# Order of the stores of weight sums in SP's queue, and a PSUM bank for each of the last two token tiles, in a float32 cross-attention block

## The chip, the cores and the metric

The kernel runs on one core of one Trainium2 chip. The metric is the device time of one execution in microseconds, as the median of several executions. A core has five engines with a queue each: TensorE (PE in the profile), VectorE (DVE, `V` in the code), ScalarE (ACT), GpSimd (POOL, `GP` in the code) and SyncE (SP), which here issues the DMAs. Within a queue instructions go in order, and between queues they wait for semaphores. Matrix products land in PSUM[...]; everything else is in SBUF.

## The reference

A transformer block on 8 sequences of 256 tokens with 512 channels: a layer norm, cross-attention with 16 heads of 32 channels on 256 encoder tokens, and a two-layer perceptron with 2048 hidden channels, all in float32. The mask is all true. The change lies in the perceptron:

```python
hidden = out + residual
residual = hidden
y = layer_norm(hidden, ln2_w, ln2_b)
y = jax.nn.gelu(y @ fc_w + fc_b, approximate=True)
y = y @ proj_w + proj_b
return residual + y
```

## The kernel before

The 2048 tokens are cut into four groups of 512 (`g` = 0 to 3). First come attention stages for all groups, with the projections of the next group laid between. Then the perceptron runs group by group (the loop at L1027). Every large product is done by a Strassen scheme with seven products of half-sized blocks in place of eight. Operands carry sums and differences of their four quarters, `11`, `12`, `21`, `22`: for weights these are `s3`, `s2`, the new `21`, and `s4` (`A_SUMS`, L155), and for tokens `t1`, `t2`, the new `12`, and `t4` (`B_SUMS`, L161). In the trace the tiles `fcw` of the first weights are called `w` or `fcw`, and all elementwise sums have the line of the helper `add`, L929; matmuls have that of `mm`, L926.

Group 0 differs from the others. Its first layer (hidden sums `pf`) runs in four quarters `q` = 0 to 3 of the hidden channels with one Strassen level (L1131 to L1200). In each quarter TensorE does the products in the order `11`, `s2`, `s3`, `21`, `12`, `22`, `s4`. They go into the PSUM banks 1, 6, 7, 5, and the last three accumulate again in banks 1, 7 and 5. VectorE and ScalarE take partial results out: `u1` is a copy on ScalarE, `u2` = bank 6 + `u1`, `u3` = bank 7 + `u2`. So product `22`, which accumulates in bank 7, has to wait until `u3` has been read out of that bank, and product `s4` until the sum `x["22"]` = bank 5 + `u3` is done. The sums `x["12"]` and `x["21"]` follow, and Gelu runs on ScalarE.

Groups 1 to 3 use a second Strassen level on the first-layer weights. The extra weight sums are made once, in group 0, beside its products, and are kept in DRAM (`w2_dram`): that is `split_sums` (L965). For a weight quarter or sum `n` and a half `r` of the columns it makes four sums `s1` to `s4` from `fcw[r]` and `fcw[r + 2]`, on VectorE or GpSimd as its first argument says. They go into one of three staging slots (`stage`, `w_stage` in the trace), used in turn, and then two DMAs on SP take them to DRAM (L979 for `s1`, L980 for the other three). A slot may be written again when the DMAs that read it have landed. With `half` 0 only the first two sums are made; with `half` 1 the other two, and then the DMAs are issued. The order is written by hand: the table `SPLITS` (L1116) says which calls come at which point `(q, at)`, and the function `splits` goes through it. A call puts its sums into its engine's queue and its two DMAs into SP's queue at that point, so SP's order is the order of the calls. Point 0 comes after `u2`, point 1 after `u3`, point 2 after `x["22"]`, and point 3 after `x["12"]`. GpSimd makes, beside its share of these sums, the sums `h` for the projection (`sum_h`) at the end of each quarter, and the roots for the next group's layer norm. The slots of `11`, `12`, `s2`, `s3`, `21`, `s4`, `22` for r = 0 are 0, 1, 2, 0, 1, 2, 0; for r = 1, `11`, `12`, `s2` take 1, 2, 0.

After the four quarters comes the projection (`py`) with seven products of 32 recorded matmuls each, from L1316: `11` into bank 1, `s3` into bank 7, then turns of the next group's tokens, then `12`, `21`, `12` with `22`, `11` with `t1`, and `22` with `t4`, which accumulates in bank 7. A bank holds two token tiles, `bank[:, 0, :]` and `bank[:, 1, :]`. In the last group the product into bank 7 at the very end is done tile by tile, so that the store of the first tile can leave before the second is done:

```python
for i in range(2):
    proj(bank[7], "22", "t4", False, True, (i,))
    o = ht[:, 2 + i, :HD2]
    add(V, o, bank[7][:, i, :], o)
    store(1, slice(HD2), (i,))
```

Of the kernel before, what the change touches and what calls it, by code (L numbers as in the profile page):

```python
# [10 lines left out]
F32 = mybir.dt.float32  # L11
# [5 lines left out]
P = 128  # L17
# [5 lines left out]
def tile_xattn_block(  # L23
# [52 lines left out]
    NG = B // GB  # L76
    G = GB * S
# [8 lines left out]
    HI, HC, HF, HD2 = INNER // 2, NC // 2, NF // 2, D // 2  # L86
# [165 lines left out]
    with ExitStack() as att:  # L252
# [5 lines left out]
        ps_m = att.enter_context(tc.tile_pool(name="ps_m", bufs=1, space=PSUM))  # L258
# [169 lines left out]
        def project_qk(g, tag):  # L428
            w, base = ("k", c_kb) if tag == "kT" else ("q", c_qb)

            def made(n, bank, u):
                o, k = int(n[0]) - 1, int(n[1]) - 1

                direct = g == 0 and o == 0
                st = None if direct else staged(g, tag, n)
                for i in range(2):
                    b = col(base, 2 * o + i)
                    to = qk[g, i, tag][:, ts(k, S)] if direct else st[:, i, :]
                    if u is None:
                        nc.scalar.activation(to, bank[:, i, :], AF.Identity, bias=b, scale=1.0)  # L440
                    else:
                        nc.vector.scalar_tensor_tensor(
                            to, bank[:, i, :], b, u[:, i, :], ALU.add, ALU.add
                        )
                if not direct:
                    store_quarter(g, tag, o, k, st)

            def src():
                return (ctxT if tag == "kT" else xnT)[g]

            if g == 0:
                for i in range(2):
                    qk[g, i, tag] = work.tile([P, G], F32, tag=tag, name=f"{tag}_{g}_{i}")
            if g == 0 and tag == "kT":
                return [lambda n=n: eight(f"p{tag}_{g}", n, ws[w], src, made, FIRST_KEYS.get(n, {})) for n in QUARTERS]
            return strassen(f"p{tag}_{g}", lambda: ws[w], src, False, made)
# [255 lines left out]
        V, GP = nc.vector, nc.gpsimd  # L712
# [53 lines left out]
        g = 1  # L766
        begin(g, 0, 3, load_res, 0, *QUARTERS)
        begin(g, 2, 2, bias_res, 0)
        g = 2
# [6 lines left out]
        g = NG - 1  # L776
# [55 lines left out]
        k, q, v, tx = project_qk(0, "kT"), project_qk(0, "qT"), project_v(0), turn_x(0)  # L832
# [63 lines left out]
        o = project_out(3)  # L896
# [11 lines left out]
    with ExitStack() as mlp:  # L908
# [5 lines left out]
        ps_m = mlp.enter_context(  # L914
            tc.tile_pool(name="ps_mm", bufs=2, space=PSUM, reuse_waits="tile")
        )
        NQF = HF // 2
        V, GP = nc.vector, nc.gpsimd
# [9 lines left out]
        def add(eng, to, a, b, op=ALU.add):  # L928
            eng.tensor_tensor(to, a, b, op)  # L929
# [97 lines left out]
        for g in range(NG):  # L1027
# [13 lines left out]
            def bank_of(n, name):  # L1041
                return ps_f.tile(
                    [P, 2, S], F32, tag=f"f{n}", bufs=2 if n in (1, 5) else 1, name=f"{name}_{g}"
                )
# [57 lines left out]
            if g == 0:  # L1102
                y = ys[g]

                def fc(bank, w, b, q, first, last):
# [9 lines left out]

                SPLITS = {  # L1116
                    (2, 0): ((GP, "11", 0), (V, "12", 0, 0)),
                    (2, 1): ((GP, "s2", 0), (V, "12", 0, 1)),
                    (2, 2): ((V, "s3", 0, 0), (GP, "21", 0)),
                    (2, 3): ((V, "s3", 0, 1),),  # L1120
                    (3, 0): ((GP, "s4", 0), (V, "22", 0, 0)),
                    (3, 1): ((GP, "11", 1), (V, "22", 0, 1)),
                    (3, 2): ((V, "12", 1, 0), (GP, "s2", 1)),
                    (3, 3): ((V, "12", 1, 1),),
                }

                def splits(q, at):
                    for args in SPLITS.get((q, at), ()):
                        split_sums(*args)

                for q in range(NQF):  # L1131
                    bank = {n: bank_of(n, f"pf{n}_{q}") for n in (1, 6, 7, 5)}
                    u1, u2, u3 = (us(n, f"u{n}_{q}") for n in (1, 2, 3))
                    x = {n: h[n][:, :, 2 * q : 2 * q + 2, :] for n in h}

                    def by_h(t):
                        return t.rearrange("p i (d s) -> p d i s", d=2)

                    def gelu(n, half, src):
                        for i in range(2):  # L1140
                            nc.scalar.activation(
                                x[n][:, :, i, :],
                                src[:, :, i, :],
                                AF.Gelu_apprx_tanh,
                                bias=col(c_fcb, half * HF + 2 * q + i),
                                scale=1.0,
                            )

                    def some_pw(n):
                        for _ in range((0, n, n // 2, n // 2)[q]):  # L1150
                            next(pw_sums)

                    fc_sums = [(1, 0), (1, 1), (1, 2), (1, 3)] if q == 0 else []
                    fc_sums += [(q + 2, i) for i in range(4)] if q + 2 < NQF else []

                    def some_fc_sums(n):
                        for at, i in fc_sums[:n]:
                            sum_up(GP, fcw[at], A_SUMS, i)
                        del fc_sums[:n]

                    fc(bank[1], "11", "11", q, True, False)
                    nc.scalar.copy(u1, bank[1])
                    fc(bank[6], "s2", "t2", q, True, True)
                    add(V, u2, bank[6], u1)
                    splits(q, 0)
                    fc(bank[7], "s3", "12", q, True, False)
                    add(V, u3, bank[7], u2)
                    splits(q, 1)
                    fc(bank[5], "21", "t1", q, True, False)
                    add(V, x["22"], by_h(bank[5]), by_h(u3))  # L1170
                    some_fc_sums(4)
                    some_pw(2)
                    splits(q, 2)
                    fc(bank[1], "12", "21", q, False, True)

                    gelu("11", 0, by_h(bank[1]))
                    gelu("22", 1, x["22"])
                    fc(bank[7], "22", "t4", q, False, True)
                    add(V, x["12"], by_h(bank[7]), by_h(u2))
                    splits(q, 3)  # L1180
                    some_norm(q, 0, 1, 1, 0)
                    some_fc_sums(4)
                    some_pw(2)
                    gelu("12", 1, x["12"])
                    fc(bank[5], "s4", "22", q, False, True)
                    add(V, x["21"], by_h(bank[5]), by_h(u2))
                    some_norm(q, 0, 1, 2, 1)
                    gelu("21", 0, x["21"])
                    sum_h("s3", q)
                    sum_h("s2", q)  # L1190
                    if q == 0:
                        ht = residual(work, hid_dram[g], "resm", f"resm_{g}")
                        load_next()
                    if q >= 1:
                        keep_quarters(q)
                    if q == 1:
                        keep_quarters(0)
                    if q == 3:
                        bias_ht()
                        normalise_next()  # L1200
# [114 lines left out]

            bank = {n: bank_of(n, f"py{n}") for n in (1, 7, 6, 5)}  # L1316

            def proj(bank, a, w, first, last, tiles=(0, 1)):
                for i in tiles:
                    for p in range(HF):  # L1320
                        mm(
                            bank[:, i, :],
                            h[a][:, i, p, :],
                            pw[w][:, p, :],
                            first and i == 0 and p == 0,
                            last and p == HF - 1,
                        )

# [14 lines left out]
            u1, u2, u3 = (us(n, f"v{n}") for n in (1, 2, 3))  # L1343
# [28 lines left out]
                    next(pw_sums)  # L1372
            proj(bank[6], "21", "t2", True, True)
            add(V, u2, bank[6], u1)
            add(V, u3, bank[7], u2)
            for b, k, u in ((0, 1, u2), (1, 1, u3), (1, 0, u2)):
                o_add(GP, b, k, u)
            if g == 0:
# [13 lines left out]
            if g + 1 < NG:  # L1392
                split_y(g + 1)
                proj(bank[7], "22", "t4", False, True)
                o_add(V, 1, 0, bank[7])
                store(1)
            else:

                store(1, slice(HD2, D))
                for i in range(2):  # L1400
                    proj(bank[7], "22", "t4", False, True, (i,))
                    o = ht[:, 2 + i, :HD2]
                    add(V, o, bank[7][:, i, :], o)
                    store(1, slice(HD2), (i,))


# [39 lines left out]
```

## Time and profile before

| what | us |
|---|---|
| median of 3 runs | 741.91 (741.21 to 742.51) |
| the profiled execution, its own time | 741.43 |
| its span in the profile | 739.7 |
| stage: group 0, first layer (`pf`) | 346.4 to 405.2 |
| stage: group 0, projection (`py`) | 405.2 to 455.3 |
| stage: groups 1 to 3 | 455.3 to 736.2 |

The span is the time that the hardware profiler shows; the execution's own time has 1.7 us more around it. Times in profile lines count from the start of the span. A timeline line has the start, the length, the engine, the line of the kernel, the operation, what it writes and reads, and in brackets how long the engine was idle before it and what ended that. "SPq" is the issue of a DMA on SP's queue. In the trace a float32 matmul of the code is two records, so a product of four matmuls is "x8".

### The profile page before, as it was taken

The page shows a single profiled execution, that of the slowest core. Times are in us where ns is not written, and L with a number is a line of the kernel's source. Part 1 is how long each engine was busy: PE and PEld are TensorE (multiplying, and loading weights), DVE is VectorE, ACT ScalarE, POOL GpSimd, SP SyncE. Part 2 cuts the span into 40 slices and gives each one's busy share as a digit, 9 for nine tenths or more (in the row PEclk, how much of TensorE's full clock was granted, in tenths as well). Part 3 has the DMA queues.
Part 4 walks back from the last instruction along what each step waited for, and adds up shares of the span by engine and source line. Part 5 has one row for each costly group of instructions (what it writes and reads, how often), then busy time and mean ns, then how long its engine had stood idle before and what let it go on. Part 6 is the DMA issues. An engine that isn't in the chain of part 4 may idle for free.

```text
span 739.7 us, 13634 instructions
## 1 busy us (share of the span) xinstructions
PE 725.8 (98%) x4941; PEld 627.5 (85%) x4941; DVE 407.2 (55%) x1055; ACT 312.4 (42%) x888; POOL 478.8 (65%) x441
## 2 busy tenths in 40 slices
PE   8999999999999999999996999999999999999997
PEld 7888788888778777778885889998899988999886
DVE  4676756666456567856466295681156811566111
ACT  2277788766676787850322200226002160031500
POOL 3857779677554479996847970489504896048960
PEclk9999999999999999999998999999999999999999
DMA  9714522642234268434965791992019930172001
GB/s 299 246 58 141 160 92 97 199 150 73 86 107 156 85 201 263 154 105 128 339 231 177 253 358 58 370 338 104 1 58 336 346 129 1 58 272 84 1 1 57
DMA packets 79714, 117.82 MB, mean 159 GB/s; under 512 B 6644, under 2 KB 58400, under 8 KB 77984
## 3 DMA queue, kind: packets, MB, share of 16 engines
q1 hardware_dynamic: 79392, 116.94, 46.1%
q8 instruction: 39, 0.64, 0.4%
q14 instruction: 27, 0.22, 0.1%
q0 software_dynamic: 256, 0.02, 0.0%
HBM read 85.48 MB, written 31.46 MB: 158 GB/s over the span
## 4 chain that ended last, share of the span: by engine, by line
PE 92%; DMA 3%; SPq 1%; POOL 1%; DVE 1%; issue 0%; ACT 0%; DVEq 0%; POOLq 0%
PE py L926 26%; PE pf L926 19%; PE ppt L628 8%; PE pv L370 7%; PE po L370 7%; PE pqT L370 7%; PE pkT L370 5%; PE s L575 5%; PE av L644 4%; PE pkT L467 2%; DMA hm<-hid_dram 1%; DMA w_dram<-w_stage 1%; PE pyt L217 1%; PE pxt L217 1%; POOL w_stage L929 1%; SPq L935 1%
## 5 line engine op out<-in xcount | busy, mean ns | idle before, releaser
L617 POOL TENSOR_TENSOR pr<-pr,rsum 128x512 f32<-128x512 f32 x128 | 130.2, 1051 | 68.7 <-DVE rsum L615 39.9
L929 POOL TENSOR_TENSOR h<-h,hs 128x512 f32<-128x512 f32 x79 | 98.8, 1273 | 105.0 <-DVE hs L929 104.4
L603 ACT ACTIVATE pr<-pr,nmax 128x256 f32<-128x256 f32 x256 | 127.8, 502 | 37.4 <-DVE nmax L593 37.1
L926 PEld LDWEIGHTS pf<-y,w 128*128 128x128 f32 x1176 | 131.8, 192 | 0.2
L926 PE MATMUL pf<-y,w 128*128 128x128 f32 x1176 | 131.8, 275 | 0.0
L593 DVE CUSTOM_DVE_ANT_0 pr<-s,mb 128x256 f32<-128x256 f32 x256 | 93.5, 413 | 39.7 <-PE s L575 29.9
L926 PE MATMUL py<-pw_t,h 128*128 128x256 f32 x384 | 84.5, 379 | 0.6 <-DVE resm L929 0.6
L926 PE MATMUL py<-pw,h 128*128 128x256 f32 x384 | 84.9, 379 | 0.0
L926 PEld LDWEIGHTS py<-pw_t,h 128*128 128x128 f32 x384 | 72.6, 190 | 10.7 <-DVE resm L929 1.0
L926 PEld LDWEIGHTS py<-pw,h 128*128 128x128 f32 x384 | 72.5, 190 | 9.6
L1267 ACT COPY u<-pf 128x512 f32<-128x512 f32 x21 | 12.3, 585 | 161.1 <-PE pf L926 161.1
L628 PEld LDWEIGHTS ppt<-ident,pr 128*128 128x128 f32 x512 | 57.5, 141 | 14.6 <-issue 9.3
L628 PE MATMUL ppt<-ident,pr 128*128 128x128 f32 x512 | 68.5, 276 | 0.2
L929 DVE TENSOR_TENSOR resm<-py,resm 128x512 f32<-128x512 f32 (+1 forms) x21 | 13.6, 663 | 85.5 <-PE py L926 85.5
L926 PE MATMUL pf<-y,fcw 128*128 128x256 f32 x224 | 52.0, 393 | 7.0 <-DVE u L929 6.6
L926 PEld LDWEIGHTS pf<-y,fcw 128*128 128x128 f32 x224 | 43.8, 197 | 15.1 <-DVE u L929 7.4
L633 ACT COPY pt<-ppt 128x512 f32<-128x512 f32 x96 | 51.8, 573 | 7.1 <-PE ppt L628 7.1
L370 PE MATMUL pv<-vw,ctxT 128*128 128x256 f32 x224 | 52.4, 380 | 0.0
L929 DVE TENSOR_TENSOR u<-pf,u 128x512 f32<-128x512 f32 x50 | 34.5, 690 | 30.9 <-PE pf L926 26.6
L370 PE MATMUL pqT<-xnT,qw 128*128 128x256 f32 x224 | 51.0, 379 | 0.0
L603 ACT ACTIVATION_READ_ACCUMULATOR pr<-pr,nmax 128x1 f32 x256 | 48.8, 191 | 0.0
L370 PEld LDWEIGHTS pqT<-xnT,qw 128*128 128x128 f32 x224 | 41.4, 190 | 5.0
(142 smaller groups left out, 1134.8 us busy)
## 6 DMA issues: line engine op xcount, KB each, us to landing
w<-w_dram SPq DMA_DIRECT2D x12, 1792.0 KB, 7.6
w<-in_L_xattn_fc_w_dram SPq DMA_DIRECT2D x27, 256.0 KB, 5.1
w<-w_dram SPq DMA_DIRECT2D x9, 768.0 KB, 7.1
w_dram<-w_stage SPq DMA_DIRECT2D x14, 384.0 KB, 3.1
ctx<-in_ctx_dram SPq DMA_DIRECT2D x16, 256.0 KB, 4.0
x<-in_x_dram SPq DMA_DIRECT2D x16, 256.0 KB, 4.9
v_dram<-st_v SPq DMA_DIRECT2D x16, 256.0 KB, 2.2
v<-v_dram SPq DMA_DIRECT2D x16, 256.0 KB, 3.6
```

What stands on the lines that cost most here:

```text
L217: nc.tensor.transpose(ps[:, ts(t, P)], xt[:, ts(c, P)], ident)
L370: nc.tensor.matmul(bank[n][:, i, :], l[:, c, ts(i, P)], r[:, c, :], start=first and i == 0 and c == 0, stop=last and c == HC - 1, skip_gro ...
L467: nc.tensor.matmul(bank[:, i, :], w[f"{n[0]}{j + 1}"][:, c, ts(i, P)], x()[f"{j + 1}{n[1]}"][:, c, :], start=at == 0, stop=j == 1 and c == ...
L575: nc.tensor.matmul(banks[j][:, i, :], qT[j * HD : (j + 1) * HD, b * S + i * P : b * S + (i + 1) * P], kT[j * HD : (j + 1) * HD, b * SK : ( ...
L593: nc.vector.tensor_tensor_reduce(pr[:, j, i, :], banks[j][:, i, :], mbias[g][1][:, b, :], scale=-SCALE, scalar=FLT_MAX, op0=ALU.add, op1=A ...
L603: nc.scalar.activation(pr[:, j, i, :], pr[:, j, i, :], AF.Exp, bias=nmax[:, j, i : i + 1], scale=-1.0, accum_out=sums[:, j, i : i + 1],)
L617: nc.gpsimd.tensor_tensor(pr[:, j], pr[:, j], rsum[:, j, :, None].to_broadcast([P, NQ, SK]), ALU.mult,)
L628: nc.tensor.transpose(ps[:, kc, ts(i, P)], probs[n][:, j, i, ts(kc, P)], ident)
L633: nc.scalar.copy(pt, ps)
L644: nc.tensor.matmul(av[j * HD : (j + 1) * HD, :], vs[g, hg][:, b * NK + kc, ts(j, HD)], pts[n, j][:, kc, :], start=(kc == 0), stop=(kc == N ...
L926: nc.tensor.matmul(ps, lhsT, rhs, start=first, stop=last, skip_group_check=True)
L929: eng.tensor_tensor(to, a, b, op)
```

## The change

In `SPLITS`, three things are altered. Where a point has a call on VectorE and one on GpSimd, and VectorE's call issues DMAs, VectorE's call now stands first, so that its two DMAs stand ahead of GpSimd's in SP's queue. `s3` of r = 0 and `12` of r = 1 are no longer made in halves at two points but whole at point 2, and point 3 with its call of `splits` is gone. The slots stay the same, and so does GpSimd's order; on VectorE two pairs of sums move ahead of one `x["12"]` each, in q = 2 and q = 3. In the last group, the two token tiles of the product that is in bank 7 get a bank each: tile 0 stays in bank 7 and tile 1 takes one from the pool `ps_m` (tag `mm`), which otherwise holds the turns of the next group's tokens. The sum `u3` of that group is then made in two instructions, one for each tile.

```diff
                 SPLITS = {
                     (2, 0): ((GP, "11", 0), (V, "12", 0, 0)),
-                    (2, 1): ((GP, "s2", 0), (V, "12", 0, 1)),
-                    (2, 2): ((V, "s3", 0, 0), (GP, "21", 0)),
-                    (2, 3): ((V, "s3", 0, 1),),
+                    (2, 1): ((V, "12", 0, 1), (GP, "s2", 0)),
+                    (2, 2): ((V, "s3", 0), (GP, "21", 0)),
                     (3, 0): ((GP, "s4", 0), (V, "22", 0, 0)),
-                    (3, 1): ((GP, "11", 1), (V, "22", 0, 1)),
-                    (3, 2): ((V, "12", 1, 0), (GP, "s2", 1)),
-                    (3, 3): ((V, "12", 1, 1),),
+                    (3, 1): ((V, "22", 0, 1), (GP, "11", 1)),
+                    (3, 2): ((V, "12", 1), (GP, "s2", 1)),
                 }
...
                     add(V, x["12"], by_h(bank[7]), by_h(u2))
-                    splits(q, 3)
...
+            last_7 = None
+            if g + 1 == NG:
+                last_7 = bank[7], ps_m.tile([P, G], F32, tag="mm", name="py7_1")[:, :HD2]
+
             def proj(bank, a, w, first, last, tiles=(0, 1)):
                 for i in tiles:
                     for p in range(HF):
                         mm(
-                            bank[:, i, :],
+                            bank[:, i, :] if last_7 is None or i == 0 or bank is not last_7[0] else last_7[1],
                             h[a][:, i, p, :],
                             pw[w][:, p, :],
-                            first and i == 0 and p == 0,
+                            first and p == 0 and (i == 0 or last_7 is not None and bank is last_7[0]),
                             last and p == HF - 1,
                         )
...
-            add(V, u3, bank[7], u2)
+            if last_7 is None:
+                add(V, u3, bank[7], u2)
+            else:
+                for i, x in enumerate((bank[7][:, 0, :], last_7[1])):
+                    add(V, u3[:, i, :], x, u2[:, i, :])
...
-                    add(V, o, bank[7][:, i, :], o)
+                    add(V, o, last_7[1] if i else bank[7][:, 0, :], o)
                     store(1, slice(HD2), (i,))
```

## The prediction

> **What bounds the kernel now.** I read the engine table of the page first, then the chain of waits between 340 and 460 us, then the timeline of each engine there, then the chain and the timeline of the last 15 us.
>
> ```profile
> PE 725.8 (98%) x4941; PEld 627.5 (85%) x4941; DVE 407.2 (55%) x1055; ACT 312.4 (42%) x888; POOL 478.8 (65%) x441
> ```
>
> TensorE is busy for 98% of 739.7 us, so an edit pays only where TensorE stands still, or runs slowly, and the change touches two such places. The chain of waits (start, length, what) shows the first:
>
> ```profile
> 382.82 2.54 DMA w_dram<-w_stage
> 385.45 0.60 DVE w_stage L929
> ...
> 386.79 3.08 DMA w_dram<-w_stage
> 390.00 0.72 POOL w_stage L929
> ...
> 391.61 1.41 POOL w_stage L929 x2
> ...
> 394.04 3.12 DMA w_dram<-w_stage
> 397.18 0.70 DVE w_stage L929
> 398.66 0.69 DVE u L929
> 399.39 5.98 PE pf L926 x16
> 405.37 13.81 PE py L926 x64
> ```
>
> For 17 us the chain leaves TensorE: a store lands, VectorE may write a staging slot, another store lands, GpSimd may write one, a third store lands, VectorE may write `22` of r=0, and only after its first two operations comes `u3` of q=3, for which the product `22` waits. The timeline shows why the third store was so late:
>
> ```profile
> 386.79 0.53 SPq L980 DMA_DIRECT2D w_dram<-w_stage  x1
> ...
> 387.43 0.42 DVE L929 TENSOR_TENSOR w_stage<-fcw,w_stage 128x256 f32<-128x256 f32 x1
> ...
> 392.29 0.73 POOL L929 TENSOR_TENSOR w_stage<-fcw,w_stage 128x256 f32<-128x256 f32 x1
> ...
> 393.05 0.37 SPq L980 DMA_DIRECT2D w_dram<-w_stage  x1
> ...
> 394.04 0.53 SPq L980 DMA_DIRECT2D w_dram<-w_stage  x1
> ```
>
> VectorE had `s3` whole at 387.85 (second line), but its store went out at 393.51 and 394.04 (its two DMAs): ahead of it in SP's queue stood the store of GpSimd's `21` (393.05). And `21` could only begin at 390.00, when the store of VectorE's `12` (386.79) had landed; that one, ready at 381.02, had itself stood behind the store of GpSimd's `s2` (385.79). The price, from the table of windows (stretch, length, PE busy, granted clock, DMA share and rate):
>
> ```profile
> 395.00:396.00 1.00, 0.00 (x0) 1.00 1.00 344
> 397.00:398.00 1.00, 0.00 (x0) 0.58 0.98 345
> 401.00:402.00 1.00, 1.00 (x4) 0.50 0.80 278
> 404.00:405.00 1.00, 1.00 (x7) 1.00 0.41 145
> ```
>
> TensorE idles, its clock falls to half near 397, and it comes back only at 404: 4 matmuls in a us, then 7. So the stall costs twice. The second place is the end:
>
> ```profile
> 731.99 0.42 DVE L929 TENSOR_TENSOR resm<-py,resm 128x256 f32<-128x256 f32 x1 [2.23 <-PE py L926]
> 732.46 3.72 PE L926 MATMUL py<-pw_t,h 128*128 128x256 f32 x16 [0.58 <-DVE resm L929]
> ```
>
> The 16 last matmuls wait until VectorE has read the first token tile out of the bank that they share.
>
> [...] (half clock about 4 us into the idle, full again 4.6 us after the restart at 399.39). [...]the stores here take 2.5 to 3.2 us from issue to landing, so an earlier issue is an earlier landing. [...] the pair of VectorE operations of a half took 0.67 us with GpSimd idle (387.09 to 387.76), 1.48 and 1.85 us with it busy (397.18, 377.28). I price with 1.48.
>
> **The change, part by part.** Times are those of the profiled execution.
>
> 1. *Stores of q=2.* After the edit SP sends, in order: `11` (V: GpSimd's, last DMA at 382.82 as now), `12` (VectorE's, ready, at about 383.3 and 383.8), `s2` (385.79 as now), `s3`, `21`. `12` lands at 383.8 + 3.1 = 386.9 and not 389.9, so GpSimd's `21` runs at 386.9 to 390.0. VectorE's `s3` still begins at 385.45 (it waits for `11`, untouched), its four operations end at 387.25, its DMAs leave at 386.95 and 387.6 and land at about 390.7. Slot 0 is then free before VectorE has done `u2` of q=3.
>
> 2. *`s3` not in halves.* Two operations, 0.67 us, go ahead of the `12` sum of the products (`x["12"]`) of q=2: it ends at 387.85, not 387.17, and product `s3` of q=3 (same bank) starts 0.7 us later. That is absorbed: product `12` of q=3 waits anyway for the copy `u1` on ScalarE at 390.69 to 391.25, which follows a VectorE sum at 389.15 that has the same work in front as before. It slips from 391.30 to about 391.4. Cost 0.1 us, of which nothing is left in step 3.
>
> 3. *The stall.* `u2` stays at 391.28. The half of `22` follows without its 5.21 us of waiting: 391.9 to 393.4. `u3` ends at 394.05, TensorE goes on at 394.1, not 399.39; its last product was through at 391.30 + 1.73 = 393.0 (8 matmuls at 0.216), so about 1.1 us of idle stay[...]. `22` runs 394.1 to 395.85; product `s4` needs the sum that reads its bank, which ends 2.47 us after `u3` began (398.66 to 401.13 now): 393.4 + 2.5 = 395.85. It ends at 397.6. The output products (`py`) began at 405.21; they begin at **397.6: 7.6 us earlier**, 5.3 from the idle, 2.3 from the clock. Bounds: with the half at 0.67 or 1.85 us, 8.4 and 7.2.
>
> 4. *What is late next.* Product `s3` of the projection needs its last quarter 6 of 16 matmul pairs in: 397.6 + 6.9 + 2.6 = 407.1. On GpSimd the norm's roots wait for the statistics (390.66), `s4` then starts at 390.7 + 3.9 = 394.6, its second DMA leaves at 398.0 and lands 2.6 later, as now: 400.6. VectorE's `12` of r=1 waits for that; from its start to the last sum of q=3 are 3.86 us (402.88 to 406.74), so 404.5, and the last Gelu ends at 405.4. GpSimd's `s2` of r=1 waits for the store of `22`, now sent right after that of `s4`: about 399.0 + 3.2 = 402.2, and 3.0 for its operations: 405.2. The sum for product `s3` ends at 405.4 + 1.3 = 406.7. That leaves 0.4 us, where it was over 2. I take no stall, up to 1 us in the range. The `s4` sums of the projection end at about 428.4 on the same count, against a need at 429.6. Loads of the next group's weights leave SP after these stores, 5 to 7 us earlier as everything here; they have tens of us in hand. From 455 to 732 TensorE is busy for 276.58 of 276.70 us, so the shift is kept to the end.
>
> 5. *(3,1), (3,2)* reorder the same way; `12` of r=1 in one piece puts 0.7 us ahead of one sum (in step 4 the whole 3.86 us is counted, so nothing is added).
>
> 6. *Two banks at the end.* 48 matmuls from 721.36 at 0.216 us are issued by 731.73; the last 16 began at 732.46. They begin **0.73 us earlier**; VectorE's last sum and the store follow as they do now. The sum `u3` of that group becomes two of 0.42 us for one of 0.69, on a VectorE that then idles for over 5 us: nothing. The other bank is one that is unused in the last group.
>
> Sum: 7.6 + 0.7 = 8.3 us. The profiled execution took 741.43, 0.48 below the median; 741.43 - 8.3 = 733.1, and about **733.6** on the scale of the median.
>
> **The rivals.**
> A. *As summed*, 732.3 to 735.5, likeliest 733.6. For it: the late store was ready 5.7 us before it left, and nothing but its place in the queue held it. Chance 0.80.
> B. *A new wait on GpSimd or on a landing takes part of it.* The slack of 0.4 us in step 4 goes; stores from the staging slots took up to 7.6 us to land, the slow ones beside large loads. With those of `s4` and `22` each 2 us later, TensorE stalls 3 to 4 us in product `s3`: about 737. Against it: none of those loads is in the queue before 406. Chance 0.10.
> C. *Only the end is gained*: if slot 0 comes free no earlier than now (landings, not places, were the limit), or TensorE stalls elsewhere for the same time, 741.2 after the 0.7. That speaks against the trace, where `s3` lay ready. Chance 0.05.
> D. *Slower.* VectorE now keeps `12` of r=1 whole in front of the sum that frees the bank of product `s3`. If GpSimd's `s4` store lands late, that sum comes 2.65 us after the landing, and TensorE stands at the bank. It decides against the change once the sum ends after 412.1 (where that product starts now) + 0.7, a landing after 410.2, that is 12 us after the issue at 398.0, where this store took 2.6; a fall of the clock beside it would make about 744. Chance 0.05.
>
> **How the numbers follow.** What a measurement here can tell from no change is about 0.2%, 1.5 us. Faster: A, B and half of C's spread, 0.92; same 0.03; slower 0.05. A's own range with B up to its centre gives 732.2 to 737.0, which leaves the rest of B, C and D, under 2 in 10, outside.
>
> **What would show it.** Right: `py` begins near 398 and the clock stays at 1.00 between 391 and 406; the DMA wait before VectorE's `22` is gone; SP sends `s3` by 388; no gap before the last 16 matmuls. Wrong: a wait of TensorE on GpSimd near 407 (B), a VectorE wait on `w_dram` still of 5 us near 392 (C), or TensorE waiting at the start of product `s3` (D).

## The result, and the profile after

On the same chip the kernel before took 742.21 us (741.21 to 742.97) and the changed one 734.12 us (732.84 to 735.45): a ratio of 0.9892 with a 95% interval of 0.9869 to 0.9914, or 8.1 us less. The forecast was 733.6 us from a sum of 8.3 us.

The profiled execution after the change took 734.6 us, with a span of 732.8 us, 6.9 us below the span of before. The chain of waits shows where it went. The same stretch of it as was shown of before (start, length, what):

```profile
383.38 2.61 DMA w_dram<-w_stage
...
386.09 0.54 DVE w_stage L929
386.72 0.44 DVE w_stage L929
387.18 0.76 DVE w_stage L929 x2
387.94 0.60 DVE h L929
...
391.98 0.69 DVE u L929
392.67 0.34 DVE w_stage L929
...
394.33 0.68 DVE u L929
...
396.68 0.61 DVE h L929
...
397.43 1.97 PE pf L926 x8
399.39 13.81 PE py L926 x64
```

Of the three landings of stores that stood in this chain only the first is left, that of GpSimd's `11`, which `s3` waits for. From `u2` of q=3 (391.98) VectorE now goes on without a pause: half of `22`, `u3`, the other half, the sum `x["22"]`. The output products follow 7.4 us after `u2` (391.98 to 399.39); before, it was 14.1 us (391.28 to 405.37).

The timeline of SP and the two other engines shows the cause. These are the last DMAs of `12`, `s2`, `s3` and `21`, and the operations beside them:

```profile
384.38 0.53 SPq L980 DMA_DIRECT2D w_dram<-w_stage  x1
...
386.37 0.37 SPq L980 DMA_DIRECT2D w_dram<-w_stage  x1
...
387.53 0.42 DVE L929 TENSOR_TENSOR w_stage<-fcw,w_stage 128x256 f32<-128x256 f32 x1
387.59 0.93 POOL L929 TENSOR_TENSOR w_stage<-fcw,fcw 128x256 f32<-128x256 f32 x1 [1.25 <-DMA w_dram<-w_stage]
...
388.05 0.40 SPq L980 DMA_DIRECT2D w_dram<-w_stage  x1
...
391.24 0.37 SPq L980 DMA_DIRECT2D w_dram<-w_stage  x1
```

`s3` was done at 387.95 (387.53 + 0.42, third line) and its last DMA left at 388.05; before, it lay ready for over 6 us. GpSimd's `21` started at 387.59, when the store of `12` had landed; its idle time there was 1.25 us, where it had been 4.24. The line of before is:

```profile
390.00 0.73 POOL L929 TENSOR_TENSOR w_stage<-fcw,fcw 128x256 f32<-128x256 f32 x1 [4.24 <-DMA w_dram<-w_stage]
```

TensorE's clock stands at 1.00 where it had been at 0.50. The table of windows (stretch, length, then busy time and instructions of PE, PEld, DVE, ACT, POOL, granted clock, DMA share, GB/s):

```profile
394.00:395.00 1.00, 0.05 (x1) 0.00 (x0) 1.00 (x3) 0.84 (x2) 0.92 (x2) 1.00 0.84 291
397.00:398.00 1.00, 0.63 (x4) 0.55 (x4) 0.88 (x2) 0.68 (x2) 0.92 (x2) 1.00 0.00 0
398.00:399.00 1.00, 1.00 (x6) 0.89 (x5) 0.00 (x0) 0.23 (x1) 1.00 (x2) 1.00 0.06 16
```

At the end, the chain of waits is one piece of matmuls to the last sum, with no VectorE in between:

```profile
681.01 48.36 PE py L926 x224
729.37 0.02 issue
729.39 0.42 DVE resm L929
```

Before, the same 224 matmuls were 208, a sum on VectorE, and the 16 that began at 732.46. The chain of before has for the first of them:

```profile
686.98 44.91 PE py L926 x208
```

With the last 16 they ran from 686.98 to 736.19 (49.21 us, now 48.36), so this part is 0.85 us shorter.

### The profile page after: what moved, and what is told of

The parts are those of the page before. It is cut to its first block, busy times and chain, and to the rows that moved or that the text cites. A ratio compares the mean times of both kernels' runs of the same rounds, so it can differ in the third digit from the quotient of the medians.

```text
span 732.8 us, 13636 instructions
## 1 busy us (share of the span) xinstructions
PE 724.0 (99%) x4941; PEld 626.1 (85%) x4941; DVE 408.5 (56%) x1056; ACT 312.6 (43%) x888; POOL 480.3 (66%) x441
## 4 chain that ended last, share of the span: by engine, by line
PE 93%; DMA 2%; DVE 2%; SPq 1%; POOL 1%; issue 1%; ACT 0%; DVEq 0%
PE py L926 26%; PE pf L926 19%; PE ppt L628 8%; PE pv L370 7%; PE po L370 7%; PE pqT L370 7%; PE pkT L370 5%; PE s L575 5%; PE av L644 4%; PE pkT L467 2%; DMA hm<-hid_dram 1%; PE pxt L217 1%; PE pyt L217 1%; SPq L935 1%; PE pct L217 1%; DMA kw<-in_L_xattn_k_w_dram 1%
## 5 line engine op out<-in xcount | busy, mean ns | idle before, releaser
L926 PE MATMUL pf<-y,fcw 128*128 128x256 f32 x224 | 49.8, 382 | 3.4 <-DVE u L929 2.2
L926 PEld LDWEIGHTS pf<-y,fcw 128*128 128x128 f32 x224 | 42.0, 190 | 11.1 <-DVE u L929 3.0
```

The source lines that it names most:

```text
L926: nc.tensor.matmul(ps, lhsT, rhs, start=first, stop=last, skip_group_check=True)
```

## The experiments

All were compared with the kernel before on the same chip as they ran. The theory: VectorE's finished stores stood behind unfinished ones of GpSimd in SP's queue, and their places there made the stall and the fall of the clock. The rivals: that the second bank brought most of it; that one of the moved calls alone counts; that the reorder in q=3 is without effect.

| run | what is changed | ratio to before, 95% | us against before |
|---|---|---|---|
| e1 | the table alone | 0.9904 (0.9891 to 0.9917) | -7.1 |
| e2 | the second bank alone | 0.9987 (0.9978 to 0.9997) | -1.0 |
| e3 | `s3` alone | 0.9997 (0.9988 to 1.0006) | -0.2 |
| e4 | `12` alone | 0.9958 (0.9946 to 0.9970) | -3.1 |
| e5 | q=2 alone | 0.9960 (0.9945 to 0.9975) | -3.0 |
| e6 | `s3`, and `22` of (3,1) | 0.9966 (0.9955 to 0.9978) | -2.5 |
| e7 | another order, two banks | 0.9882 (0.9865 to 0.9899) | -8.8 |
| e8 | the changed kernel again | 0.9897 (0.9880 to 0.9913) | -7.6 |
| e9 | a further order | 0.9884 (0.9867 to 0.9902) | -8.6 |
| e10 | e7 again | 0.9885 (0.9868 to 0.9903) | -8.5 |

The last column is the ratio less one, times the median of before in that group of runs (741.7 to 742.2 us).

### The two parts apart (e1, e2)

e1 is the changed kernel with the last group's edits taken back; e2 keeps those and takes the old table.

> The new table of SPLITS alone; the last group keeps one bank. My theory, that the stall came from the place of VectorE's store of s3 in SP's queue: the output products of group 0 begin near 399 to 399.5 us and not at 405.2, the clock stays at 1.00 there, and the time is 6 to 7.5 us below the kernel before; the gap of about 0.6 us before the last 16 matmuls stays. Rival, that the tail's bank brought most of the gain: within 2 us of before.

> The second bank alone, with the old table. My theory: 0.7 to 0.9 us below before, all of it at the last 16 matmuls, and the stall of 6.1 us with half clock behind it is untouched. Rival, that the tail's bank brought most of the gain: 4 us or more below before.

e1 gave 7.1 us (6.2 to 8.1), with the output products from 398.63 and the gap before the last 16 matmuls still there (0.59 us); e2 gave 1.0 us (0.2 to 1.6), with the last 64 matmuls in one piece. Together that agrees with the 8.1 us measured for both, closer than intervals of this width promise. In e2 the stall stands as it was, 6.09 us before product `22`, with the clock at half behind it. These are TensorE's timeline, and a window of TensorE alone (stretch, length, PE busy and instructions, granted clock, DMA share, GB/s):

```profile
399.31 6.06 PE L926 MATMUL pf<-y,fcw 128*128 128x256 f32 x16 [6.09 <-DVE u L929]
```
```profile
398.00:399.00 1.00, 0.00 (x0) 0.50 0.10 33
```

So about seven eighths of the gain come from the table of calls, and the rival of the bank falls.

### `s3` alone: the stall moves (e3)

```diff
-                    (2, 2): ((V, "s3", 0, 0), (GP, "21", 0)),
-                    (2, 3): ((V, "s3", 0, 1),),
+                    (2, 2): ((V, "s3", 0), (GP, "21", 0)),
```

> Only (2,2) is changed: s3 whole, its store ahead of GpSimd's 21; the store of 12 stays behind that of s2, and (3,1) to (3,3) are as before; one bank. My theory: the store of s3 leaves at about 387.4 and 387.9 and lands at 391, before u2 of q=3, so the stall before u3 goes as with the whole table; but GpSimd's 21 still starts near 390, its s4 near 397, the last Gelu ends near 407.5, the last sum for the product s3 of the projection near 409, and TensorE waits there 1.5 to 2.5 us: 4 to 5.5 us below before. Rival, that the chain through the store of 12 and GpSimd's 21 is what bounds: at most 1 us below before.

The first half held, the size didn't: no gain that can be told from none (0.9988 to 1.0006). The stall before product `22` was gone, and TensorE waited later, for GpSimd. TensorE's timeline of e3:

```profile
393.88 3.72 PE L926 MATMUL pf<-y,fcw 128*128 128x256 f32 x16 [0.75 <-DVE u L929]
...
412.16 1.10 PE L926 MATMUL py<-pw,hs 128*128 128x256 f32 x2 [4.54 <-POOL hs L929]
```

The 6.1 us of idle became 0.75 and 4.54, and the clock fell again behind the second (0.50 from 413 to 415). The expectation had missed that in the old order of (3,1) the store of VectorE's `22` stands behind GpSimd's `11` of r=1. `22` was ready at 394.49, and its last DMA left at 404.32, behind GpSimd's `s4` and `11`, and GpSimd's next `s2` needs that slot. GpSimd's timeline of e3:

```profile
407.56 0.73 POOL L929 TENSOR_TENSOR w_stage<-fcw,fcw 128x256 f32<-128x256 f32 x1 [4.26 <-DMA w_dram<-w_stage]
...
410.85 1.26 POOL L929 TENSOR_TENSOR hs<-h,h 128x512 f32<-128x512 f32 x1
```

The sum `hs` is ready at 412.1, and TensorE goes on at 412.16. The wait had only been passed on to the next store in SP's queue with the same fault. The time is the one that the rival named, and e3 by itself doesn't refute it: GpSimd's `21` was as late as before. e6, below, bears on it.

### `12` alone (e4)

```diff
-                    (2, 1): ((GP, "s2", 0), (V, "12", 0, 1)),
+                    (2, 1): ((V, "12", 0, 1), (GP, "s2", 0)),
```

> Only (2,1) is changed: the store of VectorE's 12 goes ahead of that of GpSimd's s2; s3 stays in halves with its store behind GpSimd's 21; one bank. My theory: 12 lands near 387, 21 runs from there to 390, the store of s3 leaves at 390.6 and 391.1 and lands near 394.2; TensorE goes on at about 396.7 after 3.6 us of idle. If the clock holds: about 5 us below before; if it falls as before: 2.5 us below. Rival, that this place is all that counts: as much as the whole table, 6 to 7.5 us below.

The two calls are on different engines, so e4 changes SP's order and nothing else: that the places in the queue cost time is shown here most directly. It gave 3.1 us (2.2 to 4.0), and the rival falls. That this is near the value expected for a clock that falls is partly luck. By the mean granted clock that is listed for each run, it held in two of the five runs (738.54 and 739.72 us) and fell in three (738.92 to 739.25), with no difference in time. In the profile GpSimd's sum for product `s3` of the projection was ready at 411.98, just before TensorE came to need it, so with a held clock TensorE would likely have waited there instead; no trace of such a run shows it. The store of `s3` left at 390.91 and 391.44 and VectorE's `22` began at 394.58, as expected, but the idle came in two pieces. TensorE's timeline and windows of e4:

```profile
393.03 1.99 PE L926 MATMUL pf<-y,fcw 128*128 128x256 f32 x8 [1.84 <-ACT u L1162]
397.40 3.04 PE L926 MATMUL pf<-y,fcw 128*128 128x256 f32 x9 [2.38 <-DVE u L929]
```
```profile
398.00:399.00 1.00, 1.00 (x6) 0.82 0.00 0
399.00:400.00 1.00, 1.00 (x4) 0.50 0.00 0
400.00:401.00 1.00, 1.00 (x4) 0.50 0.44 148
401.00:402.00 1.00, 1.00 (x4) 0.50 0.72 239
402.00:403.00 1.00, 1.00 (x6) 0.97 0.45 155
```

The first piece is for the most part the price of the halves here: with GpSimd's `21` brought forward beside it, the second half of `s3` took 1.73 us of the chain (387.42 to 389.15) where it had been 0.67. A weight sum of the projection behind it took 1.08 us and not 0.66, and everything after on VectorE, up to the `u1` copy that follows, was late.

### The reorder in q=3 (e5, e6)

e5 has the new lines of q=2 and the old ones of q=3. e6 is e3 with this besides:

```diff
-                    (3, 1): ((GP, "11", 1), (V, "22", 0, 1)),
+                    (3, 1): ((V, "22", 0, 1), (GP, "11", 1)),
```

> The changes of q=2 alone ((2,1) to (2,3)); (3,1) to (3,3) are as before; one bank. Theory after the run with s3 alone: the reorder in q=3 is what lets GpSimd follow. The output products begin near 399.4 us as with the whole table, but the store of VectorE's 22 now stands behind GpSimd's 11 of r=1: it leaves near 403 and lands near 406.2, GpSimd's s2 of r=1 starts then and not at 403.6, the last sum for product s3 of the projection ends near 410.5, and TensorE, which needs it near 408.7, waits 1.5 to 2.5 us at full clock: 4.5 to 5.5 us below before. Rival, that the reorder in q=3 is without effect: 6 to 7.5 us below, as the new table alone.

> The run with s3 whole ahead of 21, and besides (3,1) swapped: the store of 22 ahead of GpSimd's 11; the store of 12 stays behind that of s2, (3,2) and (3,3) are as before; one bank. Theory: the store of 22 leaves at about 400.8 and 401.3 and not at 403.8 and 404.3, lands near 404.4, GpSimd's s2 of r=1 starts then and not at 407.6, and TensorE's wait in product s3 of the projection falls from 4.5 us to about 1.5 us[...]: 4.5 to 6 us below before. Rival, that GpSimd's late 21 is what made it wait: at most 1.5 us below before.

In e5 the output products began at 398.33, as early as in e1, and then TensorE waited at the place named. TensorE's timeline of e5:

```profile
398.33 7.07 PE L926 MATMUL py<-pw,h 128*128 128x256 f32 x32
...
410.27 4.58 PE L926 MATMUL py<-pw,hs 128*128 128x256 f32 x20 [2.27 <-POOL hs L929]
```

The profile agrees with the theory in place and in size (2.27 us, with the clock at 1.00 from 404 to 413), and its span is 4.4 us below that of before. The time over all runs is 3.0 us below (1.9 to 4.1), less than the 4.5 expected. Between e1 and e5 only q=3's lines differ, so the reorder in q=3 is worth about 4 us (7.1 against 3.0, the fall of the clock in some runs of e5 included, see below), and that rival falls.

e6 differs from e3 in SP's order alone. It cut the wait from 4.54 to 2.90 us and not to 1.5. TensorE's timeline of e6:

```profile
411.18 4.58 PE L926 MATMUL py<-pw,hs 128*128 128x256 f32 x20 [2.90 <-POOL hs L929]
```

The stores did as expected (`22` leaves at 401.47 and 402.00), but e6's statistics and all behind ran some 0.7 us later than in e3, and `12` in halves with GpSimd beside it kept the last sum `x["21"]` and so the last Gelu to 409.8. It gave 2.5 us (1.6 to 3.3), where e3 gave none that can be told, with GpSimd's `21` as late in both: so the rival, that this `21` made TensorE wait and at most 1.5 us would come, falls, though narrowly. Whether the late `21` has a part in the 2.90 us that are left stays open.

The runs of e6 spread widely, from 736.4 to 741.6 us, and the mean granted clock that is listed for each of them accounts for most of it. Seven runs at 1.000 have a median of 738.0 us, seven at 0.998 one of 739.5, and three at 0.995 one of 741.4. The clock fell in ten of 17 runs, and the profiled one was among those where it held. A mean lower by 0.002 or 0.005 over 738 us is about 1.5 or 3.7 us of TensorE's time, and the medians are 1.5 and 3.4 us above the first. It is the same with e5: four runs at 0.999 or 1.000 took 737.1 to 738.0 us, four at 0.997 or 0.998 took 738.5 to 739.7. By the medians of the runs with the clock held, e5 gained 4.0 us and e6 3.7, so for e5 the fall of the clock is most of the shortfall. The 4.5 to 6 us expected of e6 took a held clock for granted, which was the author's estimate; in ten of its 17 runs it did not hold, with a wait in the profile twice as long as expected.

Not tested apart is what the whole sums (`s3`, and `12` of r=1) do without their new places in the queue.

### An order with the sums first (e7 to e10)

TensorE still waited 1.17, 0.86, 1.02 and 0.37 us in q=2 and q=3 of the changed kernel, always for a VectorE sum that stood behind weight sums (the first wait was 0.23 us in e8, so it differs from one execution to the next). e7 puts the sums first:

```diff
-                    (2, 0): ((GP, "11", 0), (V, "12", 0, 0)),
-                    (2, 1): ((V, "12", 0, 1), (GP, "s2", 0)),
-                    (2, 2): ((V, "s3", 0), (GP, "21", 0)),
-                    (3, 0): ((GP, "s4", 0), (V, "22", 0, 0)),
-                    (3, 1): ((V, "22", 0, 1), (GP, "11", 1)),
-                    (3, 2): ((V, "12", 1), (GP, "s2", 1)),
+                    (2, 0): ((GP, "11", 0),),
+                    (2, 2): ((V, "12", 0), (GP, "s2", 0)),
+                    (3, 0): ((V, "s3", 0), (GP, "21", 0)),
+                    (3, 2): ((V, "22", 0), (GP, "s4", 0), (GP, "11", 1), (GP, "s2", 1)),
+                    (3, 3): ((V, "12", 1),),
...
                     add(V, x["21"], by_h(bank[5]), by_h(u2))
+                    splits(q, 3)
```

> A version that may beat both: two banks, and on VectorE the sums that TensorE waits for go ahead of the weight sums. (2,0): GpSimd 11; (2,2): 12 whole, GpSimd s2; (3,0): s3 whole, GpSimd 21; (3,2): 22 whole, GpSimd s4, 11 and s2 of r=1; 12 of r=1 after the sum x21. Theory: the waits of TensorE of 1.2, 0.9, 1.0 and 0.4 us in q=2 and q=3 of the changed kernel go, the output products begin near 395.5 to 396.5 us, and the time is 2.5 to 4 us below the changed kernel. Rival: GpSimd, which is nearly full there, becomes the bound at product s3 of the projection and gives most of it back: within 1 us of the changed kernel.

> The changed kernel unaltered, for the comparison on the same chip: 7 to 9 us below before. The profile of its first run had its statistics' load land 0.6 us later than the kernel before; if that is chance, the output products begin within 0.7 us of 398.7.

e7 took 732.80 us (732.63 to 733.64) and e8, the changed kernel, 734.05 us (733.89 to 734.37) on the same chip: 1.25 us less, with no overlap of the two ranges but half of what was expected at least, and more than the rival allowed. The four waits became two. TensorE's timeline of e7:

```profile
393.05 3.72 PE L926 MATMUL pf<-y,fcw 128*128 128x256 f32 x16 [2.19 <-DVE u L929]
396.61 7.07 PE L926 MATMUL py<-pw,h 128*128 128x256 f32 x32
...
406.67 4.58 PE L926 MATMUL py<-pw,hs 128*128 128x256 f32 x20 [0.40 <-POOL hs L929]
```

`s3`, whole and with GpSimd beside it, took 4.0 us in front of `u3` (388.30 to 392.31, four operations that take 0.42 us each alone), and GpSimd was at its limit at product `s3` (0.40 us of wait), as the rival had it. The clock held in the profile of e7 (mean 1.000) with its wait of 2.19 us, but not in every run: the longest runs of e7 (733.64 us) and e10 (734.38) are the two with a mean clock of 0.997, and no trace shows where they lost it. In e8 the output products began at 398.54, so the 0.7 us by which the first profile after was late in q=2 is from one execution to the next.

e9 takes `s3` out of the way of `u3`, and GpSimd's `s2` of r=1 behind its sums for the projection:

```diff
-                    (3, 0): ((V, "s3", 0), (GP, "21", 0)),
-                    (3, 2): ((V, "22", 0), (GP, "s4", 0), (GP, "11", 1), (GP, "s2", 1)),
+                    (3, 2): ((V, "s3", 0), (GP, "21", 0), (V, "22", 0), (GP, "s4", 0), (GP, "11", 1)),
                     (3, 3): ((V, "12", 1),),
+                    (3, 4): ((GP, "s2", 1),),
...
                         sum_h("s2", q)
+                    splits(q, 4)
```

> On top of the version with the sums first: VectorE's s3 goes behind u3 and x22 of q=3, and GpSimd's s2 of r=1 goes behind the sums for the projection. (2,0): GpSimd 11; (2,2): 12, GpSimd s2; (3,2): s3, GpSimd 21, 22, GpSimd s4, GpSimd 11 of r=1; then x12, x21 and 12 of r=1; after the sums of q=3 for the projection GpSimd s2 of r=1. Theory: TensorE's wait of 2.2 us before product 22 of q=3 goes, and the one of 0.4 us on GpSimd too, as its last sum for product s3 moves from 406.6 to about 404; the output products begin near 394.5 to 395.5 us, 1 to 2.2 us below the version with the sums first. Rival: GpSimd's sums are needed 2 us earlier than before and it waits for a slot itself: the wait comes back at product s3, and the time is within 0.7 us of that version.

> The version with the sums first unaltered, for the comparison on the same chip: 8 to 10 us below before, as in its first run.

733.44 us (731.92 to 734.28) against 732.82 us (732.28 to 734.38) for e7 again: no gain, and the rival holds. All 224 matmuls of the first layer ran without a wait, and then TensorE stood for GpSimd, which had waited for a slot. TensorE's and GpSimd's timelines of e9:

```profile
347.10 48.53 PE L926 MATMUL pf<-y,fcw 128*128 128x256 f32 x224
...
407.00 4.58 PE L926 MATMUL py<-pw,hs 128*128 128x256 f32 x20 [1.87 <-POOL hs L929]
```
```profile
399.21 0.73 POOL L929 TENSOR_TENSOR w_stage<-fcw,fcw 128x256 f32<-128x256 f32 x1 [3.05 <-DMA w_dram<-w_stage]
```

So e7 has the lowest median of those run, and e9 can't be told from it. What bounds this stage now is probably the weight sums of VectorE and GpSimd together with only three slots; a fourth slot would test that, and it wasn't tried.

## Why the prediction was right

**Stores of q=2 (step 1).** Right, with its times: it had `s3` end at 387.25 and leave by 387.6, and `21` start at 386.9. The profile has 387.95, 388.05 and 387.59, 0.5 to 0.7 us later, as was that whole execution from the landing of the statistics' load in q=2 on (VectorE's first statistics there at 373.11, not 372.54). The landing of `s3` was in time: VectorE goes from `u2` (391.98, 0.69 us) to `22` (392.59) without a wait.

**`s3` in one piece (step 2).** Right: product `s3` of q=3 waited 0.86 us for the sum that frees its bank, and nothing of it was left at `u2`, which followed the `u1` copy as before; in e8, which had no late load, `u2` started at 391.28 as in the kernel before.

**The stall (step 3).** Both parts of the gain were there, the idle and the clock. That the clock would hold over the idle that stays was the author's estimate; in the profile after, it stood at 1.00 through waits of 1.17, 0.86, 1.02 and 0.37 us. Measured from `u2`, the output products began 13.93 us later before (391.28 to 405.21) and 7.25 us later after (391.98 to 399.23): 6.7 us, where 7.6 were forecast. In e8 it is 391.28 to 398.54, so 6.7 us once more. The lines of VectorE's and TensorE's timelines are, before and then after:

```profile
391.28 0.69 DVE L929 TENSOR_TENSOR u<-pf,u 128x512 f32<-128x512 f32 x1 [0.62 <-ACT u L1162]
...
405.21 7.07 PE L926 MATMUL py<-pw,h 128*128 128x256 f32 x32
```
```profile
391.98 0.69 DVE L929 TENSOR_TENSOR u<-pf,u 128x512 f32<-128x512 f32 x1 [0.63 <-ACT u L1160]
...
399.23 7.07 PE L926 MATMUL py<-pw,h 128*128 128x256 f32 x32
```

Two terms were too small: the half of `22` before `u3` took 1.74 us and not 1.48, and the time from the start of `u3` to the end of `x["22"]` 2.96 us and not 2.47. Both have VectorE's additions with GpSimd beside them (1.37 us for the one at 393.04, where one takes 0.42 alone, as at 402.53); together they are 0.75 of the 0.9 us. The bounds given were those of the first term only, so 6.7 fell outside them. e1, timed by itself, gives 7.1 us (6.2 to 8.1).

**What is late next (step 4).** The slack was right and close, though its times came 1 to 2 us later than counted, with the output products: the last sum for product `s3` ended at 408.5, against a need at 406.14 + 2.6 = 408.7. TensorE didn't stop there in the first profile; in e8 and e1 that product took 0.15 and 0.18 us longer. Rival B was thus near, and the runs showed what kept it away: the reorder in q=3, which step 5 counted as nothing of its own. Without it, e3 and e5 wait 4.54 and 2.27 us at this place in their profiles. The step reckoned with the store of `22` directly behind that of `s4`, but didn't say that this is worth about 4 us.

**Two banks (step 6).** The wait of 0.58 us is gone; the end is 0.85 us earlier in the profile, 1.0 us (0.2 to 1.6) in e2, against 0.73 forecast.

C and D didn't come about: no wait for a slot stood before `22`, and the bank of product `s3` was free when TensorE got there (the sum out of it ended at 404.35, the product started at 406.14). In sum, the mechanism held, with 0.9 us too much for the stall and a little too little for the end. By the profiles the two terms are 6.7 and 0.85, or 7.5 us, and e8, the same kernel timed again, gave 7.6 us (6.5 to 8.9). That the first measurement came as near as 8.1 us (6.4 to 9.7) to the 8.3 of the sum is in part luck.

## What to carry to other kernels

SP's queue issued its DMAs in the order of the calls, so a finished store behind an unfinished one held its buffer for as long as the other's producer needed (6.2 us for `s3` before, 9.8 us for `22` in e3). Compare, for each store on the chain of waits, when its data was ready with when it was issued. Such a place must be mended along the whole chain: e3 mended one and the next took nearly all of the gain back. Where two engines share the work beside the products, order each by who waits for it, and count what they cost each other when they run at once (here 1.37 us for a VectorE addition of 0.42).

## What the runs showed of the hardware

The length of the longest idle did not decide whether TensorE's clock fell. In the profile of e4 it fell though no idle was longer than 2.4 us (1.84 and 2.38 us with about 2 us of work between them); in the profile of e6 it held after a single idle of 2.90 us. Yet of the same two kernels two of five and seven of 17 runs have a mean clock of 1.000, and the others a lower one: one program loses the clock in some executions and keeps it in others. Where the others lost it, no trace shows.

The windows show how long it stayed down. In e4 the clocks of the five windows given above (0.82, 0.50, 0.50, 0.50, 0.97) lack 1.71 us, which is 3.42 us at half clock. Before, one window at 0.58 and six at 0.50 (397 to 404) lack 3.42 us, which is 6.84 us at half clock, twice as long. In e4 TensorE had been idle for 2.38 us until 397.40, and the fall shows only in the window from 398 to 399 (0.82), with TensorE at work again. What brings it about, no run here shows.
